# Four-layer graph network on one core: the n gate of the recurrence by seven block products instead of eight plain ones

## The chip, the cores and the metric

The kernel runs on one core of one Trainium2 chip. The metric is device time in microseconds for one execution; the times before are 1361.5, 1363.83 and 1368.96 us, median 1363.83. All data are 32-bit floats (the adjacency is 32-bit integers). The engines are named as in the profile: PE is TensorE (PEld its weight loads), DVE is VectorE, ACT is ScalarE, POOL is GpSimd, SP issues nearly all DMAs.

## The reference

Input `x` is 128 graphs x 64 nodes x 256 features, with one 64 x 64 adjacency for each graph. Four layers follow each other, each as `x = x + layer(relu(layernorm(x)))`: a graph attention with four heads, a graph attention with one head, a relational layer (whose adjacency holds only 0 and 1, so that only its loop relation counts), and three steps of a gated recurrence (GRU) in which messages go along the edges:

```
for i in range(3):
    m = einsum('bnd,de->bne', h, weight[i])
    aggr = einsum('bst,bsd->btd', A, m)
    gi = aggr @ w_ih.T + b_ih            # i_r, i_z, i_n: 256 columns each
    gh = h @ w_hh.T + b_hh               # h_r, h_z, h_n
    r = sigmoid(i_r + h_r); z = sigmoid(i_z + h_z)
    n = tanh(i_n + r * h_n)
    h = (1 - z) * n + z * h
```

## The kernel before

**Tiles.** Two graphs fill the 128 partitions; four such pairs (512 nodes) make a group, so there are 16 groups. For a group the state lies transposed, `hT`: features on partitions in two chunks of 128 (K = 2), 512 nodes along the free dimension. The product of `weight[i]` and `w_ih` is made once at the start (`wc`), so a step of the recurrence multiplies the aggregated state `aT` by `wc[i]` and the state `hT` by `whh`.

**Seven products.** A weight of 256 x 256 (two chunks in, two out) applied to 512 nodes (two halves S0 and S1 of 256) can be written as a 2 x 2 by 2 x 2 block product and done by seven block products instead of eight. The kernel does so for gates r and z together: r and z of one output chunk are the two columns of blocks. `weight_sums` (line 854) makes the sums of weight blocks once, on POOL; `state_sums` (862) makes the sums of state blocks (`hS`, `aS`) for each step, on POOL too. `Chunk.mul` (981) issues product 1 to 7 for one source (state or message). The partial sums share PSUM: 1, then 6, 5 and 3 are added one on another in the left half of bank `ry`, and after 1, 6 and 5 ScalarE copies out what stands there (`m1_there`, `m16_there`, `m165_there`, 1034 to 1041) before the next is added. Product 2 goes to the right half of bank `rz` (name `rm`), products 7 and 4 to its left half; VectorE adds these to what was copied (`r_there` 1017, `z_there` 1043). Each of these reads must be over before TensorE writes that bank again, since `half` (963) makes the whole bank the region that is touched.

**Gate n before.** `Chunk.gate` (1006) does n plainly: for each output chunk and source two products of 512 columns, into bank `nh` (from the state) and `ni` (from the message). ScalarE moves `nh` with its bias into `t` in one instruction of 512 (1014); `r_there` multiplies `t` by (1 + tanh) for a half; `n_there` (1028) adds `ni` for a half and takes the tanh; `h_there` (1049) makes the new state for a half with two VectorE operations.

**Order of the work.** Nothing is issued directly. Every call goes through `Engine` (485; its call at line 495 is the line that the profile shows for almost everything) into a `Plan`, which notes operations with an assumed cost, their dependences and buffers. `emit` (462) then runs forward and backward passes over the whole program (`PASSES`, with a random number generator of seed `SEED`): a list scheduler gives each operation a place on its engine, by due times that the backward pass made, and the best pass's order is issued. `beside` (730) issues many 64 x 64 products at once (line 736). `Banks` (1135) hands out the eight PSUM banks: one each for `ry`, `rz`, `nh` and `ni`, and four under the name `mt`, shared by everything else (transposes `tp`, `mm`, `mn`, `tq`). Steps are ordered so that two or three groups alternate, e.g. step 0 of group 2, step 2 of group 1, step 1 of group 2; the earlier layers of later groups are placed between. In the first 115 us gaps of TensorE in the plan are filled with products of a constant (`warm`, line 1550).

**Layernorm** (624, and 658 for groups from 2 on, which are transposed by DVE and DMAs instead of TensorE) takes statistics on DVE, adds epsilon on DVE, takes the power -1/2 on POOL, makes minus mean times rstd on DVE, and normalises on ACT. `elu_add` (744) has a variant for ScalarE that was switched off.

The lines that set n's products:

```
ps, new = self.bank(name)
f = 2 * D + self.c * P
nc.tensor.matmul(ps, w[:, k, f : f + P], m[:, k, :], start=new, stop=not new)
```

Of the kernel before, what the change touches and what calls it, by code (L numbers as in the profile page):

```python
# [17 lines left out]
P = 128  # L18
# [203 lines left out]
class Plan:  # L222
# [57 lines left out]
    PASSES, SEED, SPREAD = 50, 57, 50.0  # L280
# [271 lines left out]
def kernel(  # L552
# [45 lines left out]
    mhalf = nc.kept(const, [P, G], F32, name="mhalf")  # L598

# [7 lines left out]
    wsum = nc.kept(const, [P, 1 + LAYERS, 3, D], F32, name="wsum")  # L607
# [16 lines left out]
    def layernorm_T(work, psum, src, hT, natural=None, graphs=False):  # L624
# [11 lines left out]
        nc.vector.tensor_scalar(var, mv[:, :, 1], EPS, None, op0=ALU.add)  # L636
        nc.gpsimd.tensor_tensor(rstd, var, mhalf[:, :n], ALU.pow)
        hn = work.tile([P, n, D], F32, name="hn")
        nc.vector.scalar_tensor_tensor(var, mv[:, :, 0], -1.0, rstd, op0=ALU.mult, op1=ALU.mult)
        for p in range(n):  # L640
            nc.scalar.activation(
                hn[:, p, :], src[:, p, :], AF.Identity, bias=var[:, p : p + 1], scale=rstd[:, p : p + 1]
            )
# [14 lines left out]
    def layernorm_T_by_dma(work, src, hT, natural=None, graphs=False):  # L658
# [10 lines left out]
        nc.vector.tensor_scalar(var, mv[:, :, 1], EPS, None, op0=ALU.add)  # L669
        nc.gpsimd.tensor_tensor(rstd, var, mhalf[:, :n], ALU.pow)  # L670
        nc.vector.scalar_tensor_tensor(var, mv[:, :, 0], -1.0, rstd, op0=ALU.mult, op1=ALU.mult)
        hn = work.tile([P, n, D], F32, name="hn") if natural is None else natural
        for p in range(n):
            to, of = hn[:, p], src[:, p, :]
            if natural is not None:
                to, of = spread(hn[:, :, p : p + 1]), of.rearrange("p (k i b) -> p k i b", k=K, b=S)
            nc.scalar.activation(to, of, AF.Relu, bias=var[:, p : p + 1], scale=rstd[:, p : p + 1])
# [176 lines left out]
    def weight_sums(w, ws):  # L854

        r0, r1, z0, z1 = w[:, 0, :D], w[:, 1, :D], w[:, 0, D : 2 * D], w[:, 1, D : 2 * D]
        nc.gpsimd.tensor_tensor(ws[:, 0], z0, z1, ALU.add)
        nc.gpsimd.tensor_tensor(ws[:, 1], ws[:, 0], r0, ALU.subtract)
        nc.gpsimd.tensor_tensor(ws[:, 2], r1, ws[:, 1], ALU.subtract)
        nc.gpsimd.tensor_tensor(z0, r0, z0, ALU.subtract)  # L860
# [21 lines left out]
    class Recurrence:  # L882
# [57 lines left out]
        def step(self, i, back=True, in_parts=False):  # L940
# [5 lines left out]
            class Chunk:  # L946
# [3 lines left out]
                def __init__(self, c, i, hT, hnew):  # L950
                    self.c, self.i, self.hT, self.hnew = c, i, hT, hnew
                    self.banks, self.first = {}, {}
                    self.r, self.t, self.z = (work.tile([P, T], F32, name=name) for name in "rtz")
                    self.d = self.r

                def bank(self, name):

                    if name in self.banks:
                        return self.banks[name], False
                    self.banks[name] = psum.tile([P, T], F32, name=name)  # L960
                    return self.banks[name], True

                def half(self, name):

                    ps, new = self.bank("rz" if name == "rm" else name)
                    part = ps[:, S1 if name == "rm" else S0]
                    if nc.on:
                        part.region = ps.region
                    return part, new

                def begun(self, name, new):

                    if not nc.on:
                        return
                    name = "rz" if name == "rm" else name
                    if new:
                        self.first[name] = nc.ops[-1]
                    else:
                        nc.ops[-1].after.setdefault(self.first[name], False)

                def mul(self, name, q, source):

                    w, m, ms = ((whh, self.hT, hS), (wc[:, self.i], aT, aS))[source]
                    ws = wsum[:, (0, 1 + self.i)[source]]
                    cs = slice(self.c * P, (self.c + 1) * P)
# [782 lines left out]
```

## Time and profile before

| What | before |
|---|---|
| profiled execution, device time | 1364.1 us |
| its span (first to last instruction) | 1362.2 us |
| granted TensorE clock, mean | 0.998 |
| DVE instructions | 2627 |
| DMA packets, share of 16 engines (q1) | 331112, 33.6% |
| DVE stream transposes of 128x1024 | 1238 ns each |
| DVE `hn<-hn,o` 128x1024 (ELU) | 1344 ns each |
| ACT `z<-ry` copy of 128x256 | 367 ns each |
| ACT `r<-ry` activation of 128x256 | 468 ns each |
| ACT `t<-nh` activation of 128x512 | 684 ns each |
| POOL `rstd<-var,mhalf` (power, 4 elements) | 1084 ns each |

How to read the lines that follow: a group line names the source line, the engine, the operation, what it writes and reads (buffer numbers left out) and its shape, how many there were, the busy time in us and the mean duration of one in ns, and behind the second bar the engine's idle time just before them with what ended it. One 32-bit product on TensorE appears as two MATMUL and two LDWEIGHTS records. Matmuls overlap, so their durations are longer than the spacing of their starts. A line of the waits names who waited for whom, the us in total, how often, and the longest.

### The profile page before, as it was taken

The numbers are of one execution on the slowest core, as the hardware profiler recorded it, in microseconds if no ns is written. First come the engines' busy times: TensorE is split into PE (matmuls) and PEld (weight loads), VectorE is DVE, ScalarE is ACT, GpSimd is POOL, SyncE is SP. The second block draws the span as 40 slices with busy tenths as digits, with TensorE's granted clock in tenths as the row PEclk, the third lists the DMA queues.
The fourth block names the chain that finished last, engine by engine and source line by source line (L and its number), as shares of the span: only waits on it lengthen the run. The fifth ranks groups of instructions, "written<-read, shape, count | busy, mean of one in ns | idle before, by whom it ended". The sixth has DMA issues, their size and how long they took to land.

```text
span 1362.2 us, 27169 instructions
## 1 busy us (share of the span) xinstructions
PE 1338.7 (98%) x9319; PEld 928.1 (68%) x9319; DVE 1058.5 (78%) x2627; ACT 776.2 (57%) x1921; POOL 647.4 (48%) x759
## 2 busy tenths in 40 slices
PE   9999999999999999999999999999999999999996
PEld 8666767666676767667676666767666676666674
DVE  6669696977969697896968878797896969676553
ACT  4765666465565655556555665555555565555443
POOL 2444453635554373555426354463645446362632
PEclk9999999999999999999999999999999999999999
DMA  8010323434334343434334343343434333321221
GB/s 228 25 21 19 80 62 71 121 77 114 75 98 108 67 110 87 106 82 100 90 76 117 80 108 79 79 125 64 103 89 97 73 77 98 74 76 61 65 63 34
DMA packets 331819, 115.05 MB, mean 84 GB/s; under 512 B 278297, under 2 KB 324121, under 8 KB 331673
## 3 DMA queue, kind: packets, MB, share of 16 engines
q1 hardware_dynamic: 331112, 112.70, 33.6%
q8 instruction: 77, 1.26, 0.4%
q14 instruction: 70, 0.57, 0.1%
q10 hardware_dynamic: 560, 0.52, 0.1%
HBM read 51.65 MB, written 32.12 MB: 61 GB/s over the span
## 4 chain that ended last, share of the span: by engine, by line
PE 83%; DVE 9%; SPq 2%; ACT 2%; issue 2%; DMA 1%; POOL 1%; DVEq 0%; ACTq 0%
PE ry L495 22%; PE mm L495 16%; PE rz L495 16%; PE nh L495 10%; PE ni L495 10%; PE mm L736 3%; PE tp L736 3%; SPq L495 2%; DVE t L495 2%; DVE hn L495 1%; PE ni L1550 1%; PE tp L495 1%; DVE st L495 1%; DVE r L495 1%; DVE hT L495 1%
## 5 line engine op out<-in xcount | busy, mean ns | idle before, releaser
L495 POOL TENSOR_TENSOR r<-hT,t 128x256 f32<-128x256 f32 x192 | 146.1, 772 | 338.8 <-ACT t L495 338.0
L495 PE MATMUL nh<-hT,whh 128*128 128x512 f32 x384 | 194.1, 595 | 0.5 <-ACT t L495 0.5
L495 PE MATMUL ni<-aT,wc 128*128 128x512 f32 x384 | 193.8, 595 | 0.6 <-ACT aT L495 0.6
L495 ACT ACTIVATE z<-z,brz 128x256 f32<-128x256 f32 x192 | 97.1, 506 | 86.3 <-DVE z L495 85.2
L495 POOL TENSOR_TENSOR aS<-aT 128x256 f32<-128x256 f32 x96 | 75.4, 786 | 134.5 <-ACT aT L495 134.5
L495 ACT ACTIVATE t<-t,bi 128x256 f32<-128x256 f32 x192 | 92.3, 503 | 64.9 <-DVE t L495 62.7
L495 ACT COPY z<-ry 128x256 f32<-128x256 f32 x192 | 70.5, 367 | 101.1 <-PE ry L495 99.9
L495 DVE SCALAR_TENSOR_TENSOR t<-r,t 128x256 f32<-128x256 f32 x192 | 100.2, 530 | 30.9 <-ACT r L495 27.0
L495 PE MATMUL mm<-wl,hT 128*128 128x512 f32 x248 | 119.0, 593 | 0.0
L495 PE MATMUL rz<-hS,whh 128*128 128x256 f32 x384 | 116.9, 386 | 1.7 <-DVE z L495 1.4
L495 PE MATMUL ry<-hS,wsum 128*128 128x256 f32 x384 | 115.7, 383 | 1.0 <-ACT r L495 0.7
L495 DVE TENSOR_TENSOR z<-rz,z 128x256 f32<-128x256 f32 x192 | 79.8, 416 | 46.6 <-PE rz L495 36.9
L495 PE MATMUL rz<-aS,wc 128*128 128x256 f32 x384 | 115.4, 382 | 0.0
L495 PE MATMUL ry<-aS,wsum 128*128 128x256 f32 x384 | 114.8, 381 | 0.2 <-POOL aS L495 0.2
L495 ACT ACTIVATE hn<-xg,var,rstd 128x256 f32<-128x256 f32 x200 | 106.8, 591 | 14.2 <-DVE var L495 13.3
L495 DVE SCALAR_TENSOR_TENSOR r<-z,r 128x256 f32<-128x256 f32 x192 | 104.4, 556 | 12.6 <-POOL r L495 7.2
L495 DVE SCALAR_TENSOR_TENSOR hT<-r,t 128x256 f32<-128x256 f32 x192 | 106.0, 571 | 1.7 <-DVE mv L495 0.4
L495 POOL TENSOR_TENSOR hS<-hT 128x256 f32<-128x256 f32 x96 | 79.4, 830 | 56.8 <-DMA hT<-tb 30.0
L495 PEld LDWEIGHTS ry<-hS,wsum 128*128 128x128 f32 x384 | 70.6, 190 | 51.7 <-issue 26.0
L495 POOL TENSOR_TENSOR rstd<-var,mhalf 128x4 f32<-128x4 f32 (+1 forms) x70 | 73.1, 1046 | 65.0 <-DVE var L495 61.1
L495 POOL TENSOR_TENSOR xg<-xg,hn 128x1024 f32<-128x1024 f32 (+1 forms) x32 | 72.8, 2274 | 59.1 <-DVE hn L495 59.1
L495 DVE BATCH_NORM_STATS2 st<-xg 128x6 f32<-128x256 f32 x256 | 94.2, 407 | 8.0 <-POOL xg L495 5.4
(207 smaller groups left out, 3152.6 us busy)
## 6 DMA issues: line engine op xcount, KB each, us to landing
turned<-tb SPq DMA_DIRECT2D x45, 512.0 KB, 2.9
hnat<-turned SPq DMA_DIRECT2D x180, 128.0 KB, 2.7
hT<-hn SPq DMA_DIRECT2D x672, 32.0 KB, 2.0
xg<-in_x_dram SPq DMA_DIRECT2D x15, 512.0 KB, 4.6
out_dram<-xg SPq DMA_DIRECT2D x15, 512.0 KB
t<-row SPq DMA_DIRECT2D x28, 256.0 KB, 3.6
hT<-tb SPq DMA_DIRECT2D x224, 32.0 KB, 1.9
at<-in_adj_dram SPq DMA_DIRECT2D x64, 32.0 KB, 2.9
```

What stands on the lines that cost most here:

```text
L495: return do(*[real(a) for a in args], **{k: real(v) for k, v in kwargs.items()})
L736: nc.nc.tensor.matmul(*[real(x) for x in product], start=True, stop=True)
L1550: nc.spare = lambda: psum.spare and nc.nc.tensor.matmul(pause, warm, warm, start=True, stop=True)
```

## The change

- **n by sevens, for both chunks at once.** `Chunk` is replaced by `Sevens`, a chain of seven products with a bank for the sums (`sy`) and one for the products (`sz`). A step has four: n from the state, r and z of chunk 0, r and z of chunk 1, n from the message. In n's chains the two output chunks are the two block columns. n's weights get their own sums (`wsum` grows by 128 columns, `weight_sums` has a second round).
- **How n is collected.** `t` lies in the tile that becomes the new state. From the state, ScalarE puts the sums into `t` with the bias (four instructions of 256), and VectorE adds the products 2, 7 and 4. From the message VectorE adds products and sums to `t`, seven adds of 256. The two operations that make the new state, and z's tanh, are issued over 512 columns instead of two halves.
- **Banks.** `sy` has two, `sz` three, `mt` three; before `ry`, `rz`, `nh`, `ni` had one each and `mt` four.
- **Layernorm.** Epsilon and the negative mean are made on ScalarE, the product with rstd on GpSimd.
- **Other.** ELU's minimum and exponential both on ScalarE for groups from 2 on; the largest edge value is taken from the row maxima; `xg` has five buffers instead of six; another number of passes and seed of the plan.

```
-    PASSES, SEED, SPREAD = 50, 57, 50.0
+    PASSES, SEED, SPREAD = 29, 20, 50.0
...
-        nc.vector.tensor_scalar(var, mv[:, :, 1], EPS, None, op0=ALU.add)
+        nm = work.tile([P, n], F32, name="nm")
+        nc.scalar.activation(var, mv[:, :, 1], AF.Identity, bias=eps)
+        nc.scalar.mul(nm, mv[:, :, 0], -1.0)
         nc.gpsimd.tensor_tensor(rstd, var, mhalf[:, :n], ALU.pow)
-        nc.vector.scalar_tensor_tensor(var, mv[:, :, 0], -1.0, rstd, op0=ALU.mult, op1=ALU.mult)
+        nc.gpsimd.tensor_tensor(nm, nm, rstd, ALU.mult)
...
+            class Sevens:
+                def __init__(self, c, gate, sources):
+                    self.c, self.gate, self.sources, self.banks, self.first = c, gate, sources, {}, {}
+                def half(self, name):
+                    bank = "sy" if name == "y" else "sz"
+                    new = bank not in self.banks
+                    if new:
+                        self.banks[bank] = psum.tile([P, T], F32, name=bank)
+                    part = self.banks[bank][:, S1 if name == "m" else S0]
+                    if nc.on:
+                        part.region = self.banks[bank].region
+                    return part, bank, new
...
+            def from_h():
+                n = Sevens(0, "n", (0,))
...
+                seen(0, S0, n.mul("y", 1))
+                add(0, S0, n.mul("m", 2))
+                seen(1, S0, n.mul("y", 6))
+                seen(1, S1, n.mul("y", 5))
+                add(1, S1, n.mul("z", 7))
+                seen(0, S1, n.mul("y", 3))
+                add(1, S0, n.mul("z", 4))
...
+            def gates(c):
+                g = Sevens(c, "r", (0, 1))
...
+                nc.scalar.copy(r[:, S0], g.mul("y", 1))
+                nc.vector.tensor_tensor(r[:, S0], g.mul("m", 2), r[:, S0], ALU.add)
+                r_there(S0, r[:, S0])
+                nc.scalar.copy(z[:, S0], g.mul("y", 6))
+                nc.scalar.copy(z[:, S1], g.mul("y", 5))
+                z_there(S1, g.mul("z", 7))
+                r_there(S1, g.mul("y", 3))
+                z_there(S0, g.mul("z", 4))
...
+            def from_a(gated):
+                n = Sevens(0, "n", (1,))
+                def add(c, h, y):
+                    nc.vector.tensor_tensor(t[c][:, h], t[c][:, h], y, ALU.add)
+                def there(c, h):
+                    d, z = gated[c]
+                    nc.scalar.activation(t[c][:, h], t[c][:, h], AF.Tanh, bias=bi[:, 4 + c : 5 + c])
+                    nc.gpsimd.tensor_tensor(d[:, h], hT[:, c, h], t[c][:, h], ALU.subtract)
+                def done(c, h):
+                    d, z = gated[c]
+                    nc.vector.scalar_tensor_tensor(d[:, h], z[:, h], 1.0, d[:, h], op0=ALU.add, op1=ALU.mult)
+                    nc.vector.scalar_tensor_tensor(t[c][:, h], d[:, h], 0.5, t[c][:, h], op0=ALU.mult, op1=ALU.add)
+                add(0, S0, n.mul("y", 1))
+                add(0, S0, n.mul("m", 2))
+                there(0, S0)
+                add(1, S0, n.mul("y", 6))
+                add(1, S1, n.mul("y", 5))
+                add(1, S1, n.mul("z", 7))
+                there(1, S1)
+                add(0, S1, n.mul("y", 3))
+                there(0, S1)
+                done(0, both)
...
+                add(1, S0, n.mul("z", 4))
+                there(1, S0)
+                done(1, both)
...
-                return {"mt": 4, "ry": 1, "rz": 1}.get(tag, 1)
+                return {"mt": 3, "sy": 2, "sz": 3}.get(tag, 1)
...
-            xg = work.tile([P, G, D], F32, name="xg", bufs=6)
+            xg = work.tile([P, G, D], F32, name="xg", bufs=5)
...
-            elu_add(pool, src, o, nc.vector if g < 1 else nc.gpsimd, g < 0)
+            elu_add(pool, src, o, nc.vector if g < 1 else nc.gpsimd, g >= AHEAD)
```

224 lines of the change are left out of this document (71 added, 153 removed).

## The prediction

> **What bounds the kernel now.** I read the page first (busy time, then the chain that ended last), next the groups of instructions with shapes kept apart, then the timeline of TensorE alone, then the waits. The page:
>
> ```profile
> span 1362.2 us, 27169 instructions
> PE 1338.7 (98%) x9319; PEld 928.1 (68%) x9319; DVE 1058.5 (78%) x2627; ACT 776.2 (57%) x1921; POOL 647.4 (48%) x759
> PE 83%; DVE 9%; SPq 2%; ACT 2%; issue 2%; DMA 1%; POOL 1%; DVEq 0%; ACTq 0%
> ```
>
> TensorE is busy 98% of the span and holds 83% of the chain; no other engine is over 78%. A busy figure of overlapping matmuls can hide idle time, so the spacing of starts in the timeline is what counts:
>
> ```profile
> 1338.02 0.59 PE L495 MATMUL ry<-hS,wsum 128*128 128x256 f32 x2
> 1338.45 0.59 PE L495 MATMUL ry<-aS,wsum 128*128 128x256 f32 x2
> 1338.88 0.59 PE L495 MATMUL rz<-aS,wc 128*128 128x256 f32 x2
> 1339.32 1.02 PE L495 MATMUL ni<-aT,wc 128*128 128x512 f32 x2
> 1340.17 0.59 PE L495 MATMUL ry<-hS,wsum 128*128 128x256 f32 x2
> 1340.61 0.59 PE L495 MATMUL ry<-aS,wsum 128*128 128x256 f32 x2
> 1341.71 0.70 PE L495 MATMUL ry<-hT,wsum 128*128 128x256 f32 x2 [0.51 <-ACT z L495]
> ```
>
> Each product is two records. A product of 256 columns takes 0.43 us from start to start, one of 512 takes 0.86 (medians over all: 215.7 and 429 ns a record). Wherever a start comes over 12 ns later than that, I count the excess as a stall (matmuls of 256 columns or more, at L495): 38.9 us in the whole span, 22.7 of it before the products of gates r and z, 3.9 before those of n, 12.3 before the rest. So 97% of the span is columns streaming; what removes columns removes time, and what adds stalls gives it back. The groups that the change touches:
>
> ```profile
> L495 PE MATMUL nh<-hT,whh 128*128 128x512 f32 x384 | 194.1, 595 | 0.5 <-ACT t L495 0.5
> L495 PE MATMUL ni<-aT,wc 128*128 128x512 f32 x384 | 193.8, 595 | 0.6 <-ACT aT L495 0.6
> L495 PE MATMUL rz<-hS,whh 128*128 128x256 f32 x384 | 116.9, 386 | 1.7 <-DVE z L495 1.4 <-DVE r L495 0.2
> L495 PEld LDWEIGHTS rz<-hS,whh 128*128 128x128 f32 x384 | 69.8, 190 | 43.9 <-issue 23.4 <-DVE t L495 3.8 <-DVE z L495 2.8
> L495 DVE SCALAR_TENSOR_TENSOR r<-z,r 128x256 f32<-128x256 f32 x192 | 104.4, 556 | 12.6 <-POOL r L495 7.2 <-ACT z L495 5.1 <-ACT es L495 0.2
> L495 DVE TENSOR_TENSOR t<-t,ni 128x256 f32<-128x256 f32 x192 | 74.7, 413 | 15.4 <-PE ni L495 14.4
> L495 DVE SCALAR_TENSOR_TENSOR hn<-hn,o 128x512 f32<-128x512 f32 x8 | 5.9, 738 | 0.2 <-ACT hn L495 0.2
> ```
>
> nh and ni make 768 records over 48 steps: eight products of 512 columns a step. The waits show where stalls come from:
>
> ```profile
> PEld ry L495 <- ACT z L495: 26.7, 75, 1.6
> PEld ry L495 <- ACT r L495: 7.5, 23, 1.5
> PEld rz L495 <- DVE z L495: 7.0, 18, 1.0
> ```
>
> These are returns of a PSUM bank: a partial sum is read by ScalarE or VectorE before the next product may be added in the same bank. (The weight loader waits ahead of the matmul, so its 41 us are not all lost; the 22.7 us are.)
>
> **TensorE columns (removed).** Per step, 16 records x 429 ns = 6.86 us become 14 products x 2 x 215.7 ns = 6.04 us: 0.82 us less, over 48 steps **-39.6 us**. Nothing hides it: all of it lies on the bounding engine. r and z keep their 28 products a step.
>
> A 256-column record also needs a weight load. Loads of 190 ns already lie inside the 215.7 ns of the rz and ry records, so I price them at nothing; 576 more raise the loader from 928 to about 1037 us.
>
> The Trainium skill speaks against this step: "Perfetto Trace Analysis", section Matmuls, calls larger matmuls more efficient, and "TensorE: Matmul & The Clock Gate", section Back-to-back issue gap, has load and matmul together set the spacing, 81 ns at 128 columns and 131 at 512. Interpolated, an estimate from that page, 256 columns would cost 0.75 of 512, fourteen products 9.0 us against 6.9, and the sum would be near 1465 us. The rz rows, at half the spacing of the nh rows, say otherwise here.
>
> **Returns of a bank (added).** A chain of seven needs five: after products 1, 6 and 5 in the sums' bank, after 2 and 7 in the other. Today two chains a step have them, afterwards four: 10 becomes 20 a step. What counts is how many are short, that is, how much matmul work stands between the product that is read and the product that waits. I counted this in the two instruction orders, in columns at the spacing above. Today 94 returns of the r and z banks have under 1 us of cover; in the changed order 192 have. (Above, the product of 1340.61 has streamed by 1341.04, and the next of its bank begins at 1341.71: 0.67 us where the reader is free.) 22.7 us / 94 = 0.24 us each, so 192 cost 46.4: **+23.7 us**. Ends: 0 if two banks of sums hide all new ones; +58 at 0.42 us each, one product's time. I take today's price, since the readers (ScalarE copies, VectorE adds of 0.41 us) are those of today. The n products' own stalls go with them: **-3.9**.
>
> **Shared banks 4 to 3.** Attention, relations and transposes share mt; the loss of one leaves shorter cover: 16 short returns before, 31 after, at 0.24 us **+3.6** (ends 0 and 12, all of today's 12.3 again).
>
> **VectorE.** Ten adds of a half a step instead of four: +288 x 0.389 (74.7/192) = +112 us. The two operations that make h are issued over 512 columns: 192 instead of 384. Today these take 104.4 + 106.0 = 210.4; a 512-wide operation of this kind takes 0.738 (hn<-hn,o), so 142, -68 (between -68 and 0, at twice 0.55). Layernorm's two small ones leave: 26.7 + 24.4 = -51. ELU's minimum goes for 28 tiles at 0.776: -22. The second whole reduction becomes one over four values: -5. Sum 1058.5 - 34 = about 1025 us (1093 at most), 76% of the new span: free, as TensorE covers it. It would cost only where a bank's read is late, which is the range of the returns.
>
> **ScalarE.** 192 reads of nh at 0.468 (r<-ry, with a bias) for 96 at 0.684, +24; tanh of z in 96 whole instead of 192 halves, -31; 140 small layernorm operations at about 0.2 (the fd row), +28; 28 ReLUs of 1024 at 1.055, +30. Sum 827 us, 61%. **GpSimd:** 70 small products (0.11 as its smallest memset, 1.05 as its power; I take 0.25 since four elements are no more work than the memset's), +17, and 16 more weight sums at 0.51, +8; 672 us, 50%. Layernorm's chain now goes VectorE, ScalarE, GpSimd twice, ScalarE: three hand-overs as before and two small instructions more, within a microsecond, while the first statistics of a group come tens of microseconds before its products (group 15: 1071 and 1119 us). Queued behind a late bn_aggr on ScalarE are the bank reads; this too sits in the returns' range. No DMA is added. With five xg buffers instead of six a load on SP's queue waits for the store of the group five before: group 10 is stored at 1053 us, a load lands in 4.6, so 13 us remain to those statistics; without them TensorE would still have two other groups' products to stream.
>
> **Start and end.** The order holds 118 warming products for 109, put where TensorE is expected idle in the first 115 us: 9 x 0.224 = **+2.0** (ends 0 and 4). After the last product, the new tail holds a GpSimd subtraction (0.83) and two 512-wide operations where before the subtraction ran beside a tanh and two halves were done: **+0.7** (0 to 2).
>
> **Sum.** -39.6 + 23.7 - 3.9 + 3.6 + 2.0 + 0.7 = -13.5 us against the profiled execution's own 1364.1 (span 1362.2 and 1.9 around it; the median of the runs, 1363.83, is the same within 0.02%): **1350 us**, 1.0% faster. A measurement tells about 0.5%, 6.8 us, from no change.
>
> **Rivals.**
> - *The new returns are hidden.* For it: with two banks for sums and three for products, TensorE can alternate between two chains; the read is 0.4 us and two products of another chain are 0.86. Against it: the counted short covers double. Time: 1364.1 - 39.6 - 3.9 + 3.6 + 2.7 = 1327 us.
> - *The new returns cost more, and it gets slower.* Place: n's second chain, where after products 1, 6 and 5 VectorE itself adds to t before TensorE may go on, and each add also waits for the gate r of that half (tanh, then multiply). VectorE has a queue in order with pieces of 1.24 and 1.34 us (hn transposes and ELU). It decides from 0.35 us per short return: 192 x 0.35 = 67, +44.5, against -37.2 of the rest. At 0.42 us: 1385 us. Against it: today's price of 0.24 includes VectorE's reads (DVE z above).
> - *It comes to nothing.* Returns at 0.30 us (57.6, +34.9) leave -2.3: 1362 us.
> - *Columns are not the bound*, as the loads or the clock limit the halves: the start spacings and a clock of 0.998 speak against it; the time would be as in the last case or above.
>
> **Chances.** Forecast 0.54 (own range 1338 to 1359), hidden 0.18, nothing 0.12, slower 0.16. The forecast and the hidden case lie below 1357.3 but for the forecast's upper edge: faster 0.70, same 0.14, slower 0.16. The range goes from the hidden case to the near part of the slower one: 1322 to 1374.
>
> **What would show it.** Right: n's 768 records of 512 columns gone, 1344 of 256 (28 a step) in their place at 216 ns; TensorE's starts late by 60 to 65 us in sum, most before sy; VectorE near 1025 us, ScalarE 827; the loader near 1037. Wrong: spacing above 216 ns inside a run of sevens (loads), a rise of shared-bank waits past 12 us, waits of sy on VectorE's t beyond 0.35 us each, or TensorE's busy share well under 97% in the middle of the span.

## The result

Median of 20 runs 1369.37 us (1366.6 to 1373.24), beside 1363.21 us of the kernel before on the same chip: a ratio of 1.0045, 95% interval [1.0036, 1.0054]. The change makes the kernel 0.45% slower, some 6 us; that lies just within the 0.5% that I had called no change, at a chance of 0.14. The forecast was 1350 us, with 1338 to 1359 as its own range. The wide range of 1322 to 1374, drawn over most of the rivals too, holds the result, but that says little. The profiled execution of the changed kernel has a span of 1367.3 us at a mean TensorE clock of 0.993. Its page:

```profile
span 1367.3 us, 28772 instructions
PE 1324.0 (97%) x9913; PEld 1037.2 (76%) x9913; DVE 1086.8 (79%) x2556; ACT 823.4 (60%) x2089; POOL 706.0 (52%) x845
```

TensorE is busy 15 us less, and its loader is where I put it (1037). VectorE does 28 us more, where I had 34 less; GpSimd 59 us more, where I had 25. The groups of instructions, shapes kept apart, of the changed kernel:

```profile
L495 PE MATMUL sy<-aS,wsum 128*128 128x256 f32 x576 | 171.1, 382 | 3.0 <-DVE hT L495 3.0
L495 DVE TENSOR_TENSOR hT<-hT,sz 128x256 f32<-128x256 f32 x288 | 117.9, 410 | 60.2 <-PE sz L495 53.7 <-ACT hT L495 3.5 <-ACT hnat L495 1.3
L495 DVE SCALAR_TENSOR_TENSOR r<-z,r 128x512 f32<-128x512 f32 x96 | 90.6, 951 | 11.3 <-POOL r L495 6.0 <-ACT z L495 5.2
L495 DVE SCALAR_TENSOR_TENSOR hT<-r,hT 128x512 f32<-128x512 f32 x96 | 87.1, 917 | 0.5
L495 POOL TENSOR_TENSOR r<-hT,hT 128x256 f32<-128x256 f32 x192 | 156.0, 820 | 287.8 <-ACT hT L495 287.0 <-PE sy L495 0.2
L495 POOL TENSOR_TENSOR xg<-xg,hn 128x1024 f32<-128x1024 f32 x28 | 70.7, 2526 | 21.3 <-DVE hn L495 21.3
L495 POOL TENSOR_TENSOR nm<-nm,rstd 128x4 f32<-128x4 f32 x58 | 15.5, 266 | 5.5 <-ACT nm L495 1.1
```

and the same two operations of GpSimd in the kernel before:

```profile
L495 POOL TENSOR_TENSOR r<-hT,t 128x256 f32<-128x256 f32 x192 | 146.1, 772 | 338.8 <-ACT t L495 338.0
...
L495 POOL TENSOR_TENSOR xg<-xg,hn 128x1024 f32<-128x1024 f32 x28 | 67.5, 2411 | 44.8 <-DVE hn L495 44.8
```

The products of n are there in halves, and the ten adds a step cost about what I said (0.41 us each, for 0.389). But the two operations that make h last 0.917 and 0.951 us at 512 columns, not 0.738. On GpSimd only 18 us are layernorm's new products (15.5, and 2.8 for those of two elements); the subtractions, the sums of the next step, the power and the residual additions, as many as before, all last longer: +9.9, +15.5, +3.3 and +5.6 us.

**TensorE's account.** From the starts of all its records: each record's width gives it a time (429 ns for 512 columns, 215.7 for 256, and so on), and what the next start comes later than that is put to the work that starts late. My sums from the two traces (how the ends of groups of 64-wide products are priced moves the first two lines against each other by a few us):

| us | before | after | difference | forecast |
|---|---|---|---|---|
| columns and warming products | 1283.6 | 1248.7 | -34.9 | -37.6 |
| late starts of the recurrence's products | 37.1 | 58.9 | +21.8 | +19.8 |
| late starts of attention, layers, relation | 23.0 | 27.9 | +4.9 | +3.6 |
| late starts of transposes back of hT | 3.1 | 16.2 | +13.1 | within +0.7 |
| the rest | 15.4 | 15.5 | +0.1 | 0 |
| span | 1362.2 | 1367.3 | +5.0 | -13.5 |

By this account two thirds of the miss are in one line. Group 0 takes its first two steps one after the other, and group 15 its last two; there the next step needs the whole new state. The timeline of TensorE:

```profile
135.01 1.12 PE L495 MATMUL tp<-ident,hT 128*128 128x128 f32 x4 [4.77 <-DVE hT L495]
...
1334.89 1.09 PE L495 MATMUL tp<-ident,hT 128*128 128x128 f32 x4 [6.16 <-DVE hT L495]
```

Behind the last product of n now stand in line: add, tanh, GpSimd's subtraction (in the second place itself behind `xg<-xg,hnat`, 2.34 us) and two 512-wide operations for each chunk. After that wait TensorE's clock is lower. Stretches of the changed kernel (length, then the busy time of PE, PEld, DVE, ACT, POOL, the granted clock, DMA):

```profile
131.00:134.80 3.80, 0.00 (x0) 0.00 (x0) 3.80 (x12) 2.79 (x8) 2.33 (x3) 0.76 0.00 0
134.90:138.50 3.60, 3.49 (x13) 3.02 (x14) 3.02 (x9) 2.86 (x8) 3.39 (x5) 0.50 0.00 0
1328.70:1334.80 6.10, 0.03 (x1) 0.00 (x0) 2.94 (x6) 1.18 (x3) 4.29 (x4) 0.70 0.25 86
1334.80:1338.20 3.40, 3.31 (x13) 2.94 (x14) 0.54 (x1) 1.54 (x3) 3.13 (x4) 0.54 0.00 0
```

The Trainium skill has this in "TensorE: Matmul & The Clock Gate", section Why this matters for your kernels: no idle gaps beyond about 3 us between bursts of products, or the clock goes to half. The rows agree: 0.50 and 0.54 for about 3.5 us.

An account tells where TensorE waits, not what would bring the time back. The experiments are on that.

### The profile page after: what moved, and what is told of

The parts are those of the page before. It is cut to its first block, busy times and chain, and to the rows that moved or that the text cites. A ratio compares the mean times of both kernels' runs of the same rounds, so it can differ in the third digit from the quotient of the medians.

```text
span 1367.3 us, 28772 instructions
## 1 busy us (share of the span) xinstructions
PE 1324.0 (97%) x9913; PEld 1037.2 (76%) x9913; DVE 1086.8 (79%) x2556; ACT 823.4 (60%) x2089; POOL 706.0 (52%) x845
## 4 chain that ended last, share of the span: by engine, by line
## 5 line engine op out<-in xcount | busy, mean ns | idle before, releaser
L495 POOL TENSOR_TENSOR r<-hT,hT 128x256 f32<-128x256 f32 x192 | 156.0, 820 | 287.8 <-ACT hT L495 287.0
L495 DVE SCALAR_TENSOR_TENSOR hT<-r,hT 128x256 f32<-128x256 f32 (+1 forms) x288 | 182.5, 642 | 25.3 <-ACT r L495 23.9
L495 PE MATMUL sy<-aS,wsum 128*128 128x256 f32 x576 | 171.1, 382 | 3.0 <-DVE hT L495 3.0
L495 PE MATMUL sz<-hS,whh 128*128 128x256 f32 x576 | 172.6, 384 | 1.1 <-DVE hT L495 0.8
L495 PE MATMUL sy<-hS,wsum 128*128 128x256 f32 x576 | 170.1, 384 | 3.5 <-ACT r L495 2.0
L495 PE MATMUL sz<-aS,wc 128*128 128x256 f32 x576 | 166.7, 385 | 0.4 <-DVE hT L495 0.2
L495 DVE TENSOR_TENSOR hT<-hT,sz 128x256 f32<-128x256 f32 x288 | 117.9, 410 | 60.2 <-PE sz L495 53.7
L495 ACT ACTIVATE hT<-sy,bh 128x256 f32<-128x256 f32 x192 | 90.2, 470 | 78.5 <-PE sy L495 74.2
L495 PEld LDWEIGHTS sy<-aS,wsum 128*128 128x128 f32 x576 | 107.3, 190 | 29.8 <-issue 7.8
L495 ACT ACTIVATE hn<-xg,nm,rstd 128x256 f32<-128x256 f32 x200 | 107.8, 592 | 26.1 <-POOL nm L495 25.0
L495 PEld LDWEIGHTS sz<-hS,whh 128*128 128x128 f32 x576 | 106.1, 190 | 22.7 <-issue 5.2
```

Of the source, the lines that this page charges most:

```text
L495: return do(*[real(a) for a in args], **{k: real(v) for k, v in kwargs.items()})
```

## The experiments: four parts undone

Here the order of work is made anew by the plan (same seed), so each kernel differs from the changed one in more than its edit. I had three theories: the hand-overs cost the time (A), n's new returns do (B), or VectorE's queue in order does (C). All ratios are to the kernel before; the changed kernel's is 1.0045.

*Plain n in the three steps that go back by TensorE, h in halves there* (gate n as before in 3 of 48 steps):

```
-            from_h()
-            from_a([gates(c) for c in range(K)])
+            if back and nc.on:
+                all_plain()
+            else:
+                from_h()
+                from_a([gates(c) for c in range(K)])
```

> The changed kernel, but n by plain products (two of 512 columns for each chunk and source) in the three steps whose state is turned back by TensorE at once (group 0 step 0, group 15 steps 1 and 2), with the new state made in halves there. Theory A (the loss lies in the hand-over of two consecutive steps of one group, at 135 and 1335 us: 13.1 us of stalls before the transposes and 2.7 us of slower clock after them): 3 x 0.82 us of columns come back, about 15 go: near 1356 us, transposes' stall 3 us. Theory B (the loss is spread over all steps, the returns of banks cost too much): 1369 to 1372 us. Theory C (VectorE is the limit): 1369 us.

*Only tanh of z and the two operations that make h in halves in these steps:*

```
-                done(0, both)
+                for h in (S0, S1) if back else (both,):
+                    done(0, h)
```

> The changed kernel with n by sevens everywhere, but in the same three steps z's tanh and the two operations that make the new state are issued in halves of 256. Theory A: the chain after the last product loses about 1 us in each hand-over and the tail (0.95 + 0.92 us become 0.42 + 0.42), the rest of the chain stays: 1365 to 1368 us, transposes' stall still 10 us or more. Theories B and C: 1369 us.

*n's chains without returns* (the reads in the middle take the old state instead of the bank, so n is not the reference's):

```
-                add(0, S0, n.mul("y", 1))
-                add(0, S0, n.mul("m", 2))
...
+                for name, q in (("y", 1), ("m", 2), ("y", 6), ("y", 5), ("z", 7), ("y", 3)):
+                    n.mul(name, q)
+                add(0, S0, hT[:, 0, S0])
...
```

> The changed kernel with the middle reads of n's chains taken from the old state in SBUF instead of the PSUM bank, so that TensorE need not wait for them; as many ScalarE and VectorE operations as before, the sums of n are not what they should be. Theory A: stalls before the recurrence's products fall from 58.9 to about 35 us, the hand-overs keep most of theirs: 1342 to 1350 us. Theory B: the same sign but larger, below 1340. Theory C (VectorE's load is the limit): no change, 1367 to 1371 us.

*The sevens alone* (layernorm's small operations, ELU's minimum and the second maximum back on VectorE):

```
-        nc.scalar.activation(var, mv[:, :, 1], AF.Identity, bias=eps)
+        nc.vector.tensor_scalar(var, mv[:, :, 1], EPS, None, op0=ALU.add)
...
```

> The changed kernel with layernorm's small operations, ELU's minimum and the second whole reduction back on VectorE as before the change, so about 78 us more on VectorE and 57 less on ScalarE. Theory A: VectorE's load hardly matters, 1366 to 1373 us. Theory C: 1380 us or more. Theory B: in between, since reads by VectorE come later, 1372 to 1380 us.

| edit | us | ratio | interval | late starts: recurrence, transposes back |
|---|---|---|---|---|
| plain n in three steps | 1385.5 | 1.0149 | 1.0125 to 1.0174 | 78.5, 12.0 |
| halves in three steps | 1369.62 | 1.003 | 1.0014 to 1.0046 | 73.4, 5.8 |
| no returns in n | 1383.3 | 1.0136 | 1.0106 to 1.0165 | 60.8, 10.7 |
| sevens alone | 1404.25 | 1.0275 | 1.0248 to 1.0301 | 86.9, 11.8 |

The first and the third came out slower than any of the theories had it. The second run takes 10.4 us off the hand-overs and the time hardly falls (by 2 us, by the ratios): the recurrence's products are 14.5 us later. Its profiled execution, 1375.24 us, is the slowest of its ten, so a part of the 14.5 us belongs to that execution. The hand-over theory loses its support, though it is where the account shows the miss; with the order made anew it is not ruled out. In the third, n's middle reads are away and the recurrence's late starts do not fall (58.9 to 60.8). But that run doesn't test the returns cleanly either: the adds that now read the old state take 0.579 us each (336 `hT<-hT,hT`) where those that read a bank took 0.41, and VectorE is busy 1118.8 us, 32 more. The last fits the theory of VectorE's load, which had 1380 us or more: without the moves off VectorE (1149.1 us busy, 62 more) the sevens cost 2.75%. An edit in 3 of 48 steps, with the new order that came with it, cost some 14 us in the first run, so from here the order is held.

## The experiments: one engine's work at a time, the order held

In these kernels every engine issues the same instructions in the same order as in the kernel they start from; only the size of some, or the engine that runs them, is altered when they are issued. I chose the edits as the results came in.

**First four.** GpSimd's long additions in quarters, in both kernels; shorter statistics; products in the hand-over gap.

```
+                if engine == "gpsimd" and method == "tensor_tensor" and elements(args[0]) == 1024:
+                    n = args[0].shape[1] // 4
+                    for q in range(4):
+                        part = slice(q * n, q * n + n)
+                        last = do(*[a[:, part] for a in now[:3]], *now[3:])
+                    return last
```

What suggested it, in the changed kernel's timelines of VectorE, GpSimd and TensorE:

```profile
912.75 2.72 DVE L495 SCALAR_TENSOR_TENSOR hT<-r,hT 128x512 f32<-128x512 f32 x1
915.39 0.41 DVE L495 TENSOR_TENSOR hT<-hT,sz 128x256 f32<-128x256 f32 x1
...
912.12 2.80 POOL L495 TENSOR_TENSOR xg<-xg,hn 128x1024 f32<-128x1024 f32 x1
...
915.86 0.70 PE L495 MATMUL sz<-aT,wc 128*128 128x256 f32 x2 [2.02 <-DVE hT L495]
```

VectorE's operation lasts 2.72 us since GpSimd's addition runs until 914.92; the add behind it, a return of a bank, is late, and TensorE waits 2.02 us. "SBUF — State Buffer" of the Trainium skill, section SBUF: two separate sides, calls this an exclusive lock between the two engines, held for a whole instruction; the rows agree.

> The changed kernel with its order of work kept on every engine; only GpSimd's 43 additions of 1024 columns in SBUF (the residual after a layer, xg<-xg,hn, and after a recurrence, xg<-xg,hnat; 2.5 us each) are issued as four of 256 columns. Theory H (held operations): in the changed kernel 9 of the recurrence's VectorE operations r<-z,r and hT<-r,hT last over 2 us instead of 0.6 to 0.95 (2.72 us at 912.75 beside a GpSimd addition of 2.80 us, after which the program runs 2.1 us later against its own order's timing than before it); VectorE and GpSimd do not run such operations side by side, and the long addition holds VectorE, which is then late for TensorE. By H no operation of this kind lasts over 1.6 us any more, and the time falls by 5 to 12 us, to 1357 to 1364. Theory C (VectorE's load as such is what costs, wherever it comes from): GpSimd's work stays and grows by some 43 x 3 x 0.2 = 26 us, VectorE's shares of waiting stay, the time is within 3 us of 1369. Theory A (only the two hand-overs between consecutive steps of one group cost): no change there, within 2 us.

> The same edit (GpSimd's additions of 1024 columns as four of 256) on the kernel before, order of work kept. There 14 of the recurrence's VectorE operations last over 2 us (2.57 at 267.46, 724.89, 745.29 and 1068.83). Theory H: the gain is there too, since the holds are as many, but less of it reaches TensorE, which waits on half as many short returns: 3 to 8 us less, 1355 to 1360. Theory C and theory A: within 3 us of 1363.

```
-            nc.vector.bn_stats(st[:, p, :], src[:, p, :])
+            nc.vector.bn_stats(st[:, p, :], src[:, p, : D // 4])
```

> The changed kernel, order of work kept on every engine; bn_stats reads 64 of a row's 256 columns instead of all, so mean and variance are of a quarter of the row (this part of the computation is changed). VectorE's 256 operations of 0.407 us become about 0.2 us each: some 50 us less of its 1087, spread over the span and none of it in the recurrence's chain. Theory C (VectorE is in TensorE's loop: it is busy 97% or more in 465 of the 1210 us of the steady part, and TensorE's lost time there doubled against before, 15.8 to 31.5 us): 8 to 15 us less, 1354 to 1361, and the loss in those stretches falls to about 20. My prediction's view (VectorE is covered by TensorE): within 3 us of 1369. Theory A: within 3 us. Theory H: holds stay, 2 to 6 us less.

```
+                for _ in range(18):
+                    nc.nc.tensor.matmul(real(pt)[:, 0, :], one, one, start=True, stop=True)
```

> The changed kernel, order of work kept; 18 products of 128 x 128 with the unit matrix (some 4.0 us, results never read) stand before the first of the transposes that follow a step whose next step is the same group's, into the bank that these transposes then fill: TensorE has work in the 5 and 6 us in which it waits for hT at 135.0 and 1334.9. Theory A with the clock: after each of these waits the granted clock was 0.50 and 0.54 for 3.5 us, which is some 1.7 us lost each; with the products it stays at 1.00, and the time falls by 2.5 to 4 us, to 1365 to 1367, while the waits for hT stay (they become busy time). If the clock is not lowered by the wait, or the products are themselves late: within 1.5 us, or up to 2 us slower.

The quarters give 1.011 [1.009, 1.0129] in the changed kernel and 1.0022 [1.001, 1.0034] in the one before: slower in both. No operation of the recurrence lasts over 1.3 us any more, and VectorE's busy time falls by 22.0 and 20.3 us; GpSimd's rises by 25.4 in both, since a quarter takes 0.73 us and four 2.9:

```profile
L500 POOL TENSOR_TENSOR xg<-xg,hn x112: 713/728/1223, 123.6 to 1214.1; 128x256 f32<-128x256 f32 x112
```

So shortening the long holds gained nothing, and theory H falls; whether GpSimd's 25 us hid a gain is answered with the prices below. The short statistics take 38.3 us off VectorE and give 1.0027 [1.0016, 1.0038]: 2.5 us. Theory C, which had 8 to 15 us, falls as well, and "VectorE is covered" is nearly right for this kind of work.

The products in the gap do keep the clock (the same stretch of 134.9 to 138.5 us, now at 1.00):

```profile
134.90:138.50 3.60, 3.60 (x79) 2.97 (x78) 3.30 (x11) 3.56 (x10) 3.51 (x5) 1.00 0.12 18
```

and yet the ratio is 1.0057 [1.0037, 1.0078], no better. TensorE is 2.0 us earlier than in the changed kernel at 197 us, 0.9 at 724 (where it now waits 1.41 us for `hT<-tb`, 0.65 in the changed kernel), and 0.3 us later at 1062. The chain that ended last shows how at 724, in this run (start, length, what):

```profile
709.25 1.08 ACT aT L495 x2
710.33 0.07 issue
710.40 0.74 POOL aS L495
711.13 0.07 issue
711.20 0.74 POOL aS L495
...
721.47 0.62 SPq L495
722.09 0.04 issue
722.14 1.96 DMA hT<-tb
724.10 0.35 issue
724.44 0.67 PE sy L495 x2
```

From 711.9 to 722.1 SyncE issues 16 DMAs, at 0.65 us from one to the next; they, not TensorE, set when that step may begin. Here a part of TensorE's gain ends, since another engine is the last to be ready. It need not be the only such place. The chain's shares, first of this run, then of the run that follows below with less work on GpSimd (the page of the changed kernel itself has none):

```profile
PE 59%; DVE 14%; SPq 9%; POOL 7%; ACT 5%; issue 4%; DMA 2%; DVEq 0%; POOLq 0%; ACTq 0%
```

```profile
PE 85%; DVE 5%; SPq 4%; ACT 2%; POOL 2%; issue 2%; DMA 1%; ACTq 0%; DVEq 0%; POOLq 0%
```

It was 83% in the kernel before. The share moves much from one run to another, so it is a hint and no measure.

**Second four.** The same 40 us of columns out of either kernel, half of GpSimd's additions out, and a new order.

```
+                        if nc.on and q == 6 and self.gate == "r":
+                            half_of(nc.ops[-1], ps, lhsT, rhs, new, stop)
...
+            to, of = real(ps)[:, :P], real(rhs)[:, :P]
+            return nc.nc.tensor.matmul(to, real(lhsT), of, start=new, stop=stop, skip_group_check=True)
```

> The changed kernel, order of work kept on every engine; product 6 of the chains of the gates r and z (sy<-hS,wsum and sy<-aS,wsum of the gates) streams 128 of its 256 columns, so the gates' second half is not what it should be: 48 steps x 2 chunks x 2 sources = 192 products, 0.431 us each, at 0.219 us, which takes 40.7 us of columns off TensorE and nothing off any other engine. Theory T (TensorE's columns still set the time of the changed kernel, with some loss on top): 28 to 40 us less, 1329 to 1341. Theory D (the saved columns of the change are no longer on the path: a program in which every engine follows a fixed order is now held by the chain over VectorE, GpSimd, ScalarE and SyncE's queue, which took 40% of the chain that ended last, 17% before): 5 to 20 us less, 1349 to 1364.

> The same edit on the kernel before, order kept: product 6 of the gates' chains (ry<-hS,wsum and ry<-aS,wsum) on 128 of its 256 columns, the same 40.7 us of columns. Theory T: 30 to 41 us less, 1322 to 1333, the same as in the changed kernel within 5 us. Theory D: clearly more than in the changed kernel, 25 to 38 us less, 1325 to 1338.

```
+                if engine == "gpsimd" and method == "tensor_tensor" and elements(args[0]) == 1024:
+                    part = slice(0, args[0].shape[1] // 2)
+                    return do(*[a[:, part] for a in now[:3]], *now[3:])
```

> The changed kernel, order kept; GpSimd's additions of 1024 columns (residuals of the layers and of the recurrences) add 512 of them, so half of each residual is left out: 43 operations of 2.55 us become about 1.3, some 52 us less of GpSimd's 706. The additions as quarters had made GpSimd 25 us longer and the time 13 us longer, although no operation of VectorE was held over 1.3 us any more. Theory G (GpSimd's queue, in order, is in the chain of each step: subtraction and sums of the next step stand behind the additions): 8 to 20 us less, 1349 to 1361. Theory V (VectorE alone, by its load): within 3 us of 1369; VectorE's shorter statistics, 38 us less of work, had given 1.5.

```
-    PASSES, SEED, SPREAD = 29, 20, 50.0
+    PASSES, SEED, SPREAD = 14, 4, 50.0
...
+        return (405.0 if bias and scale else 300.0 if bias else 215.0) + 0.73 * n
...
```

> The changed kernel with tanh of z and the two operations that make h issued in halves in the three steps whose state goes back by TensorE, the plan's costs of ScalarE's and GpSimd's operations set to what the trace has (normalisation 0.592 us for 0.497, power 1.07 for 1.00, small products 0.26 for 0.21, activations without a bias 0.1 less), and another order of work (another seed). All of the change's savings and returns are there. Theory P (any two orders of the same operations differ by some us, and the shipped order of the changed kernel is not a good one): 1352 to 1362, below the kernel before. Theory D or G with no part for the order: 1364 to 1370, as in the run with halves before.

40 us of TensorE's columns are worth 17 us in the kernel before (0.9875 [0.9841, 0.991]) and 7 in the changed one (0.9993 [0.9972, 1.0014]): theory T falls in both, theory D's difference is there; the 7 us lie in D's range, the 17 below it. By the account of TensorE's starts, the late starts of the recurrence's products grow by some 18 us in the kernel before and by some 26 in the changed one, when 40 us of columns go. The chain that ended last, of the kernel before with fewer columns:

```profile
PE 48%; DVE 26%; SPq 11%; ACT 4%; issue 4%; DMA 4%; POOL 3%; DVEq 0%; ACTq 0%; POOLq 0%
```

Less GpSimd, 53.2 us by its busy time, is worth 17 us (0.992 [0.9897, 0.9943]), as theory G had it. By the account some 12 of these are late starts of the recurrence's products, only about 1 is at the hand-overs. The other order with halves is no better (1.0041 [1.0026, 1.0055]); that the order kept was a bad one, theory P of that run, got no support.

**Third four.** The control on the kernel before; then whether it comes back with the whole computation.

The edit of the control is that of half the additions.

> The kernel before, order of work kept; GpSimd's additions of 1024 columns add 512 of them, so half of each residual is left out: 43 operations of 2.3 to 2.4 us become about 1.3, some 48 us less of GpSimd's 647. In the changed kernel this edit took 16 us off. Theory G1 (GpSimd became a bound only with the change, whose 59 us more of GpSimd used up the room): 0 to 6 us less, 1357 to 1363. Theory G2 (GpSimd's work costs about a third of its length in both kernels): 12 to 18 us less, 1345 to 1351; then the 59 us that the change adds to GpSimd would by themselves be worth some 18 us.

```
+                    n = args[0].shape[1] // 2
+                    plan.nc.vector.tensor_tensor(*[a[:, n:] for a in now[:3]], *now[3:])
+                    return do(*[a[:, :n] for a in now[:3]], *now[3:])
```

> The changed kernel with its order kept; in the place of each of GpSimd's 43 additions of 1024 columns, VectorE adds the last 512 columns and GpSimd the first 512; the whole sum is computed. GpSimd some 52 us less (of 706), VectorE some 27 us more (of 1087). Theory G (GpSimd's queue sets the time): 8 to 16 us less than 1369, 1353 to 1361, below the kernel before. Theory V (VectorE and GpSimd count alike, or VectorE more): 0 to 5 us less, 1364 to 1369.

> The same sharing of the 43 additions in the kernel before, order kept: GpSimd some 48 us less of 647, VectorE some 25 more of 1059. Theory G1: within 4 us of 1363. Theory G2: 8 to 16 us less, 1347 to 1355.

```
+        op.call = lambda: nc.nc.vector.tensor_tensor(real(nm), real(nm), real(rstd), ALU.mult)
```

> The changed kernel, order kept; the 70 small products -mean * rstd of layernorm (nm<-nm,rstd, four elements, 0.26 us each) are issued on VectorE in the places where GpSimd had them: GpSimd 18 us less, VectorE some 12 to 25 more. It undoes one of the moves of the change. Theory G: a third of GpSimd's 18 us, 4 to 8 us less, 1361 to 1365. Theory V: 0 to 4 us more.

The control gives 0.996 [0.9946, 0.9974], 5.5 us: theory G1. Sharing the additions is slower in both kernels, 1.013 [1.0113, 1.0147] and 1.0054 [1.0038, 1.0071], and so is the return of layernorm's products to VectorE, 1.0159 [1.0142, 1.0176]. I had these three the wrong way round. What they have in common, as I read it, is an operation that VectorE cannot start at once. In the run with shared additions, VectorE and GpSimd:

```profile
124.34 1.60 DVE L498 TENSOR_TENSOR xg<-xg,hn 128x512 f32<-128x512 f32 x1
...
124.13 1.27 POOL L499 TENSOR_TENSOR xg<-xg,hn 128x512 f32<-128x512 f32 x1
```

and the moved product (shortest, median, longest, in ns):

```profile
L627 DVE TENSOR_TENSOR nm<-nm,rstd x70: 147/164/2310, 6.5 to 1261.0; 128x4 f32<-128x4 f32 x58, 128x2 f32<-128x2 f32 x12
```

The first waits out GpSimd's half; the second waits for GpSimd's power (VectorE idle 11.8 us in 17 places). Both stand in VectorE's line in front of the reads of TensorE's banks. VectorE's busy time rises by 17.8 and 17.0 us, GpSimd's falls by 41.8 and 18.6, and the time rises by 11.6 and 15.5: that is hardly a price per microsecond of work. That it is waiting in line was not tested apart.

**Last two.** Attention's weights on half of their columns, and the one version that might beat both.

```
+            part = (slice(None),) * (len(to.shape) - 1) + (slice(0, N // 2),)
+            return nc.nc.vector.tensor_tensor(real(to)[part], real(to)[part], real(other)[part], alu)
```

> The changed kernel, order kept; the three VectorE operations of the attention on the weights t (t<-t,gd, t<-t,fd, t<-t,mt; operands in SBUF) work on half of their columns, so half of the attention's weights are not the right ones: VectorE 40 to 50 us less of 1087, none of it in a recurrence. The statistics (bn_stats) gave 2.5 us for 38 us of VectorE by the ratios to the kernel before; they last 0.377 to 0.431 us whatever GpSimd does, while t<-t,fd lasts 0.257 to 2.83 us. Theory P (what binds is the work of VectorE and GpSimd that excludes the other's, both on operands in SBUF): 8 to 18 us less, 1351 to 1361. Theory V (VectorE's load alone, at the statistics' price): 2 to 4 us less, 1365 to 1367.

```
-            elu_add(pool, src, o, nc.vector if g < 1 else nc.gpsimd, g < 0)
+            elu_add(pool, src, o, nc.vector if g < 1 or g % 2 else nc.gpsimd, g < 0)
```

> The kernel before with the residual additions of every second group on VectorE instead of GpSimd, the plan's costs of ScalarE's and GpSimd's small operations set to what the trace has, and its own order of work (another seed). The whole computation. Some 14 operations of 2.3 us leave GpSimd and become 1.1 us on VectorE. If the exclusion of the two engines is what costs in this kernel too (theory P), a plan that shares the additions saves some of it: 1355 to 1361. Otherwise within 4 us of 1363, or slower, as the sharing of every addition in the old order was.

0.9988 [0.9974, 1.0002], 7.8 us, between the two theories. VectorE's busy time fell by 30.0 us only, and GpSimd's by 12.5 with it; at the price of the next section GpSimd's part is 4 us, which leaves some 4 for VectorE's. It leans to theory P and doesn't settle it. The second is the same as before, 1.0007 [0.9997, 1.0017]. No version here beats both kernels.

## What a microsecond of each engine costs

From the kernels that keep the order, the busy time taken or added (for TensorE the columns, by the account) and the time it moved, as the ratio less that of the kernel it starts from, times 1364 us. By the intervals of the ratios each time is uncertain by 2 to 5 us, and the changed kernel's own ratio is that of the first section, taken at another time:

| engine, edit | work | before: time | changed: time |
|---|---|---|---|
| TensorE, product 6 on half | some -40 us each | -17.1 (0.43) | -7.1 (0.18) |
| GpSimd, half additions | -45.9, -53.2 | -5.5 (0.12) | -17.1 (0.32) |
| GpSimd, quarters | +25.4, +25.4 | +3.0 (0.12) | +8.9 (0.35) |
| VectorE, short statistics | -38.3 | not run | -2.5 (0.07) |

GpSimd's two edits agree with each other within each kernel, one adding and one taking away, while VectorE's busy time falls in all four (by 20 to 27 us); solved together, the two edits give GpSimd 0.12 before and 0.33 after the change, and VectorE's fall nothing (0.00 and -0.02). So it is GpSimd's work, or what waits for it or stands behind it in its queue, and not VectorE's holds. The change turned the prices round: TensorE 0.43 to 0.18, GpSimd 0.12 to 0.33. In between lies the result, as an estimate from these rows. The 34.9 us of columns are worth 6 to 15 us, the 58.6 us of GpSimd cost 7 to 19, VectorE's 28.3 some 2 at the statistics' price: from 6 us less to 15 more, measured 6 more. That range holds the result but also no change at all; it shows that such prices can turn the gain into a loss, not that they did. Nor does a glance at the stretches settle it. Four of them, before and after (the work in them is not the same):

```profile
885.00:900.00 15.00, 15.00 (x99) 10.19 (x101) 12.78 (x26) 7.43 (x18) 8.26 (x10) 1.00 0.60 158
900.00:915.00 15.00, 15.00 (x143) 9.98 (x136) 14.89 (x35) 6.83 (x14) 11.31 (x12) 1.00 0.35 100
975.00:990.00 15.00, 15.00 (x171) 9.83 (x170) 15.00 (x31) 7.63 (x16) 9.34 (x11) 1.00 0.30 56
990.00:1005.00 15.00, 15.00 (x54) 9.87 (x53) 14.89 (x44) 9.22 (x22) 7.48 (x8) 1.00 0.31 100
```

```profile
885.00:900.00 15.00, 15.00 (x99) 12.50 (x98) 15.00 (x31) 8.17 (x20) 12.38 (x11) 1.00 0.53 153
900.00:915.00 15.00, 13.84 (x150) 10.99 (x148) 14.97 (x31) 8.45 (x16) 9.31 (x9) 1.00 0.28 61
975.00:990.00 15.00, 14.89 (x183) 11.92 (x182) 14.95 (x32) 8.87 (x20) 7.75 (x9) 1.00 0.46 117
990.00:1005.00 15.00, 14.11 (x57) 10.48 (x57) 14.96 (x32) 7.76 (x20) 12.35 (x13) 1.00 0.36 94
```

TensorE was busy throughout beside a nearly full VectorE; now it is idle for 0.9 us of 15 where GpSimd is at 12.35, for 1.2 where GpSimd is at 9.31, less than before, and not at all where GpSimd is at 12.38.

Two things stay open. Why GpSimd's work costs three times as much now was not taken apart: its subtraction stands in the chain that makes h, its sums in front of the next step, other engines wait for the additions themselves, and it excludes VectorE; the runs lessened all of these at once. And the prices hold for a kept order; whether a new order would make more of 40 us of columns was not tried.

## Why the prediction was wrong

- **"Nothing hides it: all of it lies on the bounding engine"** (columns, -39.6) is the step that failed. The columns went (34.9 to 37.6 us, by how the 64-wide products are priced), but 40 us of columns are worth 17 us in the kernel before, where its order is kept, and 7 in the changed one; nearly half in the one and over half in the other comes back as late starts of the recurrence's products. TensorE busy 98%, and 83% of the chain, is not TensorE alone: the chain goes through the other engines as soon as TensorE is faster (48% in the kernel before with 40 us of columns less).
- **GpSimd, 672 us and 50%**, was costed at nothing, with no cover named but "within a microsecond" for layernorm. It is 706: the 18 us of new products as said, but 34 us of old operations that became longer, which I had not priced. At 0.12 to 0.33 the 59 us in all are worth 7 to 19 us, an estimate, beside a miss of 19.
- **VectorE, 1025 us (1093 at most), "free, as TensorE covers it"**: 1086.8, near the bound. The two 512-wide operations at 0.738 came from too small a row: 8 in all, seven of 0.66 to 0.69 us and one of 1.15. At 0.934, in 192, that is +38. "Free" is fair for statistics (0.07), and it seems false for what waits in line ahead of a bank's read.
- **Returns, +23.7 - 3.9**: +21.8 measured in the account, so the size was right, with some luck in its make-up: of 261 late starts of n's, r's and z's products (after 256 or 512 columns), 168 are 0.09 to 0.12 us late (before: 114 of 157). Nearly all of these are the second record of a product whose first came late or directly behind 64-wide products (110 of the 168, before 93 of the 114), as in the prediction's line of 1341.71, 0.70 us for 0.59. Those behind 64-wide products are no return of a bank: of the 22.7 us that the price of 0.24 was made from they are 7.6. That the returns bound the time was not shown; the run without n's middle reads was slower, in another order and with slower adds.
- **Shared banks, +3.6**: 4.9. **Loader, 1037**: 1037.2, spacing 216 ns, so the halves cost no more per column than the whole. The sum "near 1465 us" by the skill's spacings takes 1364.1 and the columns alone; with the prediction's other terms (+26) it is some 1490. **ScalarE 827**: 823.4.
- **Start and end, +2.7**: of the sum's terms this is the one that was mis-sized most. It had 0.7 us for the tail and nothing for the two hand-overs between steps of one group, which hold 13 us of the account. In the run with halves 10 us of them went, and came back in the recurrence, in another order; what they cost with the order held was not measured. With products in the gap the clock stayed at 1.00 there, and that gave no time back.
- Of the rivals "it gets slower" has the sign; its place was VectorE's queue in order, its price 0.35 us and more for each short return, and GpSimd, whose work has a price in these runs, was in none of them. Why the changed kernel is 6 us slower, and not merely less fast than forecast, stays open: the prices allow it and don't show it.

## What to carry to other kernels

Where all engines follow one fixed order and the first of them is 97% busy, a microsecond saved on it isn't a microsecond: measure its price by taking some columns out with the order held, and the price of the engines that the change loads, before adding up a sum. An engine at 50% can be dear, as GpSimd was here. And work that goes from one engine to another can cost more than it saves where it has to wait in its new queue: sharing the additions took 42 us off GpSimd, put 18 on VectorE and made the changed kernel 12 us slower.

## What the runs showed of the hardware

- After TensorE had stood idle for 4.8 and 6.2 us, its granted clock was 0.50 to 0.54 for about 3.5 us; with small products in the gap it was 1.00.
- A VectorE addition of 512 columns in SBUF that started 0.2 us after one of GpSimd (1.27 us) took 1.60 us; the shortest such additions took 0.68. The statistics last 0.377 to 0.431 us whatever runs beside them.
- Where a product of the recurrence comes behind 64-wide products or after a wait, its second record often starts 0.104 us later than the usual 0.216 us; two thirds of the late starts counted above are of this size.
- In the stretch shown, SyncE issued 16 DMAs in a row at 0.65 us from one to the next, 10.2 us in all.
